# Moving row moments behind the residual sums, and splitting the normalization's apply over two engines, in the first stage of a decoder kernel

## The chip, the cores and the metric

The kernel runs on one core of a Trainium2 chip. The metric is the device time of one execution in microseconds. Each kernel is timed several times; the profile is one further execution, recorded by the hardware profiler.

The engines are named as the profile names them: PE is TensorE (matrix products; PEld its weight loads), DVE is VectorE, ACT is ScalarE, POOL is GpSimd, SP is SyncE, which issues most of the DMAs. Each engine runs its instructions in the order in which they were queued. An instruction that must wait holds up all that is queued behind it on the same engine, and nothing on the others.

## The reference

The program is a decoder of two layers with normalization after each residual sum. Four sequences ("batches") of 512 tokens and width 256 are carried through six blocks, all in float32. Only the first block matters here:

```
K, V, Q = x @ theta_K.T, x @ theta_V.T, x @ theta_Q.T
for each token in order:                      # W, b start at W0, b0
    g = (2/256) * (W @ k + b - v)
    W = W - 0.01 * outer(g, k);  b = b - 0.01 * g
    out = W @ q + b
x = layernorm(x + out)                        # mean and variance over the 256 columns, eps 1e-5
```

The five blocks behind it (attention over a context of 1601 tokens, a routed mixture of eight experts, causal self attention, cross attention with rotary positions, and a dequantized feed-forward block) read that `x`. None of their code is touched.

## The kernel before

A sequence of 512 tokens is held as four tiles of 128 tokens on 128 partitions: `x[b]` is 128 x 4 x 256. `xT[b]` is its transpose, which products need as an operand.

The first stage is the generator `ttt(b)`. The token loop is turned into triangular products over tiles of 128 tokens. One call of the generator runs to its next `yield`, and queues a small piece of work:

- call 1: `to_xT`, eight transposes on PE (L188) and one ACT copy out of PSUM (L196);
- calls 2 and 3: `kT` and `qT`, eight 512-column products each (L202), then an ACT copy (L300);
- calls 4 to 7: for each tile i, the products of kT with kT and qT (fewer columns with each i), a DVE instruction into `gh` (L316), and two POOL instructions (L317, L318);
- call 8: two DVE instructions that start `inv` (L323, L324);
- calls 9 to 20: six levels of inverting the triangular blocks; the first call of a level transposes `inv` (L329), copies it (L331), and masks a product into `mid` (L336), the second adds a product to `inv` (L343);
- calls 21 to 28: for each tile j two calls. The odd one queues a product into `rs` (L367), and, for j > 0, `out_of(j-1)`: a product whose residual sum `r[:, j-1]` is made by DVE (L357). The even one queues the short product of `inv` with `rs`, copied by ACT into `z` (L373);
- call 29: `out_of(3)`, then `normalize`: four `bn_stats` (L107), four `bn_aggr` (L109), a square root on ACT (L98), a reciprocal (L100) and four `tensor_scalar` (L116), all but the root on DVE;
- call 30: `to_xT` of the normalized tiles, for the next stage.

The addition of `b0b` to `x[b]` (L305) is queued on POOL in call 4, but depends only on the transposes of call 1, so POOL may run it early.

The order of the stage is written out by hand: under `manual_schedule` the program order is the queue order. The loop at the end of the stage takes at most two generators forward in turns, one call each per turn, the older first. The second generator starts after the seventh turn, the third after the first has ended, the fourth after the second. In the order so made, the end of the first batch (A) stands with calls 22 and 23 of the second (B), the end of B with calls 6 and 7 of C, the end of C with calls 22 and 23 of D, and D ends alone.

PSUM holds in this stage two double-bank tiles (`wide`, for the transposes and the wide products) and four single banks (`bank`). The tiles of pool `p1` have two buffers, one for each of the two batches under way.

The second stage begins with small products of weights (`w`, `w2T`), then the queries from `xT[0]`. The loads of the next weights are queued on SP behind the end of the first stage, because they reuse its memory. The third to sixth stages follow, PE being the busiest engine in all of them. In a later stage `normalize_apart` normalizes in another way: a DVE instruction makes `nb` = -mean x rstd (L166), and ACT applies scale and shift with Identity (L171).

Of the kernel before, what the change touches and what calls it, by code (L numbers as in the profile page):

```python
# [9 lines left out]
F32 = mybir.dt.float32  # L10
I32 = mybir.dt.int32
BF16 = mybir.dt.bfloat16
AF = mybir.ActivationFunctionType
ALU = mybir.AluOpType
# [3 lines left out]
P = 128  # L18
B, S, D = 4, 512, 256
S2 = 1601  # L20
NT = S // P
# [18 lines left out]
def decoder(ctx: ExitStack, tc: tile.TileContext, a: dict, out: bass.AP):  # L40
    nc = tc.nc

    persist = ctx.enter_context(tc.tile_pool(name="persist", bufs=1))
    small = ctx.enter_context(tc.tile_pool(name="small", bufs=4))
# [10 lines left out]
    def wide():  # L55
        return psum["A"].tile([P, 2, 512], F32, tag="wide", name="wide")

    def bank():
        return psum["B"].tile([P, 512], F32, tag="bank", name="bank")


    x = [persist.tile([P, NT, D], F32, tag=f"x{b}", name=f"x{b}") for b in range(B)]
# [7 lines left out]
    eps5 = persist.tile([P, 1], F32, tag="eps5", name="eps5")  # L70
# [24 lines left out]
    def rstd_of(mv, eps, n=NT):  # L95

        sd = small.tile([P, NT], F32, tag="sd", name="sd")[:, :n]
        nc.scalar.activation(sd, mv[:, :, 1], AF.Sqrt, bias=eps)  # L98
        rs = small.tile([P, NT], F32, tag="rstd", name="rstd")[:, :n]
        nc.vector.reciprocal(rs, sd)  # L100
        return rs

    def moments(r, n=NT):
        st = small.tile([P, NT, 6], F32, tag="st", name="st")
        mv = small.tile([P, NT, 2], F32, tag="mv", name="mv")[:, :n]
        for t in range(n):
            nc.vector.bn_stats(st[:, t, :], r[:, t, :])  # L107
        for t in range(n):
            nc.vector.bn_aggr(mv[:, t, :], st[:, t, :])  # L109
        return mv  # L110

    def normalize(dst, r):
        mv = moments(r)
        rs = rstd_of(mv, eps5)
        for t in range(NT):
            nc.vector.tensor_scalar(  # L116
                dst[:, t, :], r[:, t, :], mv[:, t, 0:1], rs[:, t : t + 1], ALU.subtract, ALU.mult
            )
# [76 lines left out]
    def to_xT(b):  # L195
        nc.scalar.copy(xT[b], transposed(x[b]))  # L196

    def mm(ps, terms):

        n = len(terms)  # L200
        for i, (l, r) in enumerate(terms):
            nc.tensor.matmul(ps, l, r, start=(i == 0), stop=(i == n - 1))  # L202
# [12 lines left out]
    with (  # L215
# [71 lines left out]
        def bc4(t):  # L287
            return t[:, None, :].to_broadcast([P, NT, P])

        def ttt(b):  # L290

            to_xT(b)
            yield
            kq = []
            for n, w in (("kT", thK), ("qT", thQ)):
                ps = wide()
                for o in range(2):
                    mm(ps[:, o, :], [(w[:, c, o * P : (o + 1) * P], xT[b][:, c, :]) for c in range(2)])
                t = p1.tile([P, 2, S], F32, tag=n, name=n)
                nc.scalar.copy(t, ps)  # L300
                kq.append(t)
                yield
            kT, qT = kq

            nc.gpsimd.tensor_tensor(x[b], x[b], b0b[:, None, :].to_broadcast([P, NT, D]), ALU.add)  # L305


            gh = p1.tile([P, NT, 2, S], F32, tag="gh", name="gh")
            dg = p1.tile([P, NT, P], F32, tag="dg", name="dg")
            for i in range(NT):  # L310
                blk = slice(i * P, (i + 1) * P)
                n = slice(i * P, S)
                ps = wide()
                for w, t in enumerate((kT, qT)):
                    mm(ps[:, w, n], [(kT[:, c, blk], t[:, c, n]) for c in range(2)])
                nc.vector.tensor_scalar(gh[:, i, :, n], ps[:, :, n], 1.0, -CSTEP, ALU.add, ALU.mult)  # L316
                nc.gpsimd.tensor_copy(dg[:, i, :], gh[:, i, 0, blk])  # L317
                nc.gpsimd.tensor_tensor(gh[:, i, 1, blk], gh[:, i, 1, blk], lev[:, NLEV, :], ALU.mult)  # L318
                yield


            inv = p1.tile([P, NT, P], F32, tag="inv", name="inv")
            nc.vector.tensor_tensor(inv, dg, bc4(lev[:, 0, :]), ALU.mult)  # L323
            nc.vector.tensor_tensor(inv, inv, bc4(ident), ALU.add)  # L324
            yield
            for l in range(1, NLEV):
                pt = bank()
                for j in range(NT):
                    nc.tensor.transpose(pt[:, j * P : (j + 1) * P], inv[:, j, :], ident)  # L329
                back = p1.tile([P, NT, P], F32, tag="back", name="back")  # L330
                nc.scalar.copy(back, pt.rearrange("p (j q) -> p j q", q=P))  # L331
                pa = bank()
                for j in range(NT):
                    mm(pa[:, j * P : (j + 1) * P], [(dg[:, j, :], inv[:, j, :])])
                mid = p1.tile([P, NT, P], F32, tag="mid", name="mid")
                nc.vector.tensor_tensor(  # L336
                    mid, pa.rearrange("p (j q) -> p j q", q=P), bc4(lev[:, l, :]), ALU.mult
                )
                yield
                pc = bank()  # L340
                for j in range(NT):
                    mm(pc[:, j * P : (j + 1) * P], [(back[:, j, :], mid[:, j, :])])
                nc.vector.tensor_tensor(inv, inv, pc.rearrange("p (j q) -> p j q", q=P), ALU.add)  # L343
                yield

            z = p1.tile([P, NT, D], F32, tag="z", name="z")
            rs = p1.tile([P, NT, D], F32, tag="rs", name="rs")
            r = p1.tile([P, NT, D], F32, tag="r", name="r")

            def out_of(j):  # L350
                ps = bank()
                mm(
                    ps[:, :D],
                    [(qT[:, c, j * P : (j + 1) * P], w0T[:, c, :]) for c in range(2)]
                    + [(gh[:, i, 1, j * P : (j + 1) * P], z[:, i, :]) for i in range(j + 1)],
                )
                nc.vector.tensor_tensor(r[:, j, :], ps[:, :D], x[b][:, j, :], ALU.add)  # L357

            for j in range(NT):
                blk = slice(j * P, (j + 1) * P)  # L360
                ps = bank()
                mm(
                    ps[:, :D],
                    [(xT[b][:, c, blk], merged[:, c, :]) for c in range(2)]
                    + [(gh[:, i, 0, blk], z[:, i, :]) for i in range(j)],
                )
                nc.vector.tensor_tensor(rs[:, j, :], ps[:, :D], b0b, ALU.add)  # L367
                if j > 0:
                    out_of(j - 1)
                yield  # L370
                ps = bank()
                mm(ps[:, :D], [(inv[:, j, :], rs[:, j, :])])
                nc.scalar.copy(z[:, j, :], ps[:, :D])  # L373
                yield
            out_of(NT - 1)
            normalize(x[b], r)
            yield
            to_xT(b)

        ordered.enter_context(tc.manual_schedule())  # L380
        going, waiting, turn = [ttt(0)], [1, 2, 3], 0
        while going:
            for g in list(going):
                if next(g, going) is going:
                    going.remove(g)
            turn += 1
            if waiting and len(going) < 2 and turn >= 7:
                going.append(ttt(waiting.pop(0)))
            if turn == 9:
                clear_rows()  # L390
# [237 lines left out]
    with tc.tile_pool(name="p2", bufs=2) as p2, ExitStack() as ordered:  # L628
# [175 lines left out]
        for i in range(len(steps) + 1):  # L804
            if i + 1 < len(steps):
                b, t = steps[i + 1]
# [11 lines left out]
            if i > 0:  # L818
                b, t = steps[i - 1]
# [1220 lines left out]
```

## Time and profile before

| What | Value |
|---|---|
| Time, three runs | 2365.4, 2371.91, 2372.49 us (median 2371.91) |
| The profiled execution | 2369.97 us, its span 2367.9 us |
| Mean granted PE clock of the span | 0.972 |
| First stage, start to the last transposes | 0 to about 242 us |
| PE busy in 0 to 242 us | 208.41 us |
| DVE, ACT, POOL busy in 0 to 242 us | 81.33, 38.46, 23.22 us |

The span is the time between the first and the last instruction in the profile. "Busy" counts running instructions only. The granted clock is the share of full speed that PE's clock was given: at 0.50 every product takes twice as long. In a timeline line the columns are start (us), duration (us), engine, line, operation, output<-input, shapes, count, and in brackets the engine's idle time before it and what ended that.

### The profile page before, as it was taken

Reading aid. Unit: us, or ns where it says so; the run is one execution under the profiler, and the core shown is the slowest. Engines: PE = TensorE matmul, PEld = TensorE weight load, DVE = VectorE, ACT = ScalarE, POOL = GpSimd, SP = SyncE. Lnnn points to the kernel's source line nnn. Section 1 sums busy time; section 2 is a strip of 40 time slices with the busy share of each in tenths; the row PEclk is TensorE's granted clock in tenths of the full one; section 3 lists DMA queues with packets and bytes.
Section 4 is the critical chain, followed back from the end, with each engine's and each line's share of the span. In section 5 each row is a group of like instructions: output and inputs, shape, how many; then the busy total and the mean of one; then the engine's idle time right before and its main releaser. Section 6 shows DMA issues by size and latency. Waiting matters only on the chain.

```text
span 2367.9 us, 36132 instructions
## 1 busy us (share of the span) xinstructions
PE 2271.9 (96%) x14440; PEld 1287.9 (54%) x14440; DVE 1233.4 (52%) x2918; ACT 1064.2 (45%) x2103; POOL 371.2 (16%) x383
## 2 busy tenths in 40 slices
PE   7899999989999999889999999999999999999998
PEld 4768577768989889633333344333333333333366
DVE  1433334442343443565666676667776776777234
ACT  1111222224555455334555534656656565666730
POOL 1010001121222223426120000211112010000000
PEclk9999999989999999889999988999999999999999
DMA  8400311127877777343131210111110010101000
GB/s 303 181 0 1 134 56 46 46 108 247 348 296 279 282 275 285 112 151 89 60 114 57 84 37 1 42 54 48 69 34 29 25 60 20 60 1 28 23 9 27
DMA packets 77099, 244.13 MB, mean 103 GB/s; under 512 B 11640, under 2 KB 34686, under 8 KB 64638
## 3 DMA queue, kind: packets, MB, share of 16 engines
q1 hardware_dynamic: 59310, 140.39, 17.1%
q0 software_dynamic: 13632, 89.32, 10.0%
q10 hardware_dynamic: 3984, 12.05, 1.5%
q8 instruction: 116, 1.90, 0.3%
q14 instruction: 57, 0.47, 0.1%
HBM read 196.12 MB, written 56.77 MB: 107 GB/s over the span
## 4 chain that ended last, share of the span: by engine, by line
PE 54%; DMA 1%; DVE 1%; ACT 1%; POOL 1%; SPq 0%; issue 0%; DVEq 0%; POOLq 0%; ACTq 0%
PE s L1472 24%; PE one L202 12%; PE po L1499 12%; PE s L202 3%; PE s L1482 1%; PE one L1457 1%; DMA kcd<-in_c_rowkc 1%; PE one L1520 1%; ACT x L171 0%; ACT ex L1486 0%; DMA y<-ys,yrows 0%; DMA cx<-in_ctxT 0%; DVE pm L1429 0%; DVE one L1431 0%; PE one L1541 0%
## 5 line engine op out<-in xcount | busy, mean ns | idle before, releaser
L1486 ACT ACTIVATE ex<-s 128x512 f32<-128x512 f32 (+1 forms) x1062 | 578.2, 594 | 462.4 <-PE s L1472 227.7
L1429 DVE TENSOR_REDUCE pm<-one 128x1 f32<-128x512 f32 x768 | 493.6, 685 | 163.7 <-PE s L1472 107.5
L1472 PE MATMUL s<-q,kc 32*128 32x512 f32 x1612 | 531.2, 641 | 0.8 <-ACT ex L1486 0.8
L202 PE MATMUL one<-kc,qt 32*128 32x512 f32 (+1 forms) x2048 | 485.3, 565 | 0.3 <-DVE pm L1429 0.3
L1472 PEld LDWEIGHTS s<-q,kc 32*128 32x128 f32 x1612 | 166.8, 179 | 204.3 <-issue 172.4
L1499 PE MATMUL po<-ex,v 128*32 128x256 f32 (+3 forms) x2688 | 251.7, 443 | 0.3 <-ACT ot L1512 0.3
L1431 DVE CUSTOM_DVE_ANT_0 one<-one,c_diagq 128x512 f32<-128x512 f32 x256 | 171.9, 716 | 86.1 <-PE one L202 76.6
L1499 PEld LDWEIGHTS po<-ex,v 128*32 128x32 f32 (+1 forms) x2688 | 54.1, 108 | 253.1 <-issue 246.4
L1472 PE MATMUL s<-q,ks 32*128 32x512 f32 x512 | 179.5, 656 | 12.0 <-DVE q L1461 7.2
L202 PEld LDWEIGHTS one<-kc,qt 32*128 32x128 f32 x2048 | 164.9, 189 | 11.7 <-DVE pm L1429 7.9
L202 PE MATMUL one<-ks,qt 32*128 32x512 f32 x512 | 148.2, 656 | 0.0
L202 PE MATMUL bank<-eWo,g 128*128 128x256 f32 x608 | 138.8, 384 | 8.7 <-DVE rb L995 5.4
L202 PE MATMUL wide<-xbT,eWg 128*128 128x128 f32 (+1 forms) x960 | 138.9, 305 | 2.1 <-ACT g L973 2.1
L202 PE MATMUL wide<-xbT,eWi 128*128 128x128 f32 (+1 forms) x960 | 138.7, 305 | 0.9 <-DMA eWi<-in_eWi 0.9
L975 DVE TENSOR_TENSOR g<-g,sg 128x1024 f32<-128x1024 f32 x38 | 46.4, 1223 | 174.5 <-ACT sg L973 165.6
L202 PEld LDWEIGHTS wide<-xbT,eWi 128*128 128x128 f32 x960 | 129.5, 192 | 9.7 <-issue 2.1
L202 PEld LDWEIGHTS wide<-xbT,eWg 128*128 128x128 f32 x960 | 129.8, 194 | 8.9 <-ACT g L973 2.3
L1304 POOL TENSOR_TENSOR raw<-raw,c_cos 128x512 f32<-128x512 f32 (+1 forms) x32 | 35.0, 1095 | 632.5 <-DVE swp L1303 632.5
L202 PEld LDWEIGHTS bank<-eWo,g 128*128 128x128 f32 x608 | 114.4, 192 | 27.8 <-DVE rb L995 9.4
L1472 PEld LDWEIGHTS s<-q,ks 32*128 32x128 f32 x512 | 53.5, 187 | 90.0 <-issue 70.6
L202 PE MATMUL wide<-ctxT,q 128*128 128x512 f32 (+1 forms) x256 | 91.3, 510 | 0.8 <-DVE q L669 0.8
L973 ACT ACTIVATE g<-wide,eWi 128x128 f32<-128x128 f32 (+1 forms) x240 | 72.8, 411 | 38.9 <-PE wide L202 38.1
(346 smaller groups left out, 2955.1 us busy)
## 6 DMA issues: line engine op xcount, KB each, us to landing
xs<-zero SPq DMA_DIRECT2D x32, 512.0 KB
kc<-kcd SPq DMA_DIRECT2D x16, 800.5 KB
eWo<-in_eWo SPq DMA_DIRECT2D x8, 1408.0 KB
eWi<-in_eWi SPq DMA_DIRECT2D x8, 1028.0 KB
eWg<-in_eWg SPq DMA_DIRECT2D x8, 1028.0 KB
qt<-qd SPq DMA_DIRECT2D x32, 256.0 KB
ctxT<-in_ctxT SPq DMA_DIRECT2D x4, 1601.0 KB
kcd<-raw SPq DMA_DIRECT2D x24, 256.0 KB
```

What stands on the lines that cost most here:

```text
L202: nc.tensor.matmul(ps, l, r, start=(i == 0), stop=(i == n - 1))
L973: nc.scalar.activation(dst[:, k, :], pv[:, k, :], func, bias=bias)
L975: nc.vector.tensor_tensor(part, part, dst, ALU.mult)
L1304: eng.tensor_tensor(raw[:, :n], raw[:, :n], cos[:, :n], ALU.mult)
L1429: nc.vector.tensor_reduce(pm[:, t, j, c : c + 1], ps, AX.X, ALU.max)
L1431: nc.vector.tensor_tensor_reduce(out=ps, in0=ps, in1=diagq[:, 384 - t * P : 896 - t * P], scale=1.0, scalar=LOWEST, op0=ALU.add, op1=ALU.m ...
L1457: nc.tensor.transpose(pt[:, t * P : (t + 1) * P], ng.rearrange("p j r -> p (j r)"), ident)
L1472: nc.tensor.matmul(ps[:kn], kt[rows, k * P : k * P + kn], q2[rows, :], start=True, stop=cross)
L1482: nc.tensor.matmul(ps[:, k * P : (k + 1) * P], later_[:, :P], later_[:, P:], start=False, stop=True)
L1486: nc.scalar.activation(ex[:kn, h, :], ps[:kn], AF.Exp)
L1499: nc.tensor.matmul(state["po"][j * 32 : j * 32 + 32, q0:q1], (vals if cross else vself)[b % 2][:kn, k, c0 : c0 + 32], ex[:kn, j % 2, q0:q1 ...
L1520: nc.tensor.transpose(pt[:, t * P : (t + 1) * P], ot[:, t * P : (t + 1) * P], ident)
```

## The change

It touches only `ttt(b)`:

1. The `bn_stats` of a tile stands in `out_of`, right behind the residual sum of that tile. Its tile `st` comes from pool `p1`.
2. A `yield` stands between `out_of(3)` and the rest of the normalization, so that each generator has 31 calls in place of 30: 29 is `out_of(3)`, 30 the rest of the normalization, 31 `to_xT`.
3. The rest of the normalization is written out. The four `bn_aggr`, the square root and the reciprocal stay; DVE adds one small instruction, `nb`. Tiles 0 and 1 are shifted and scaled by ACT with Identity, tiles 2 and 3 by DVE as before.

```
                 nc.vector.tensor_tensor(r[:, j, :], ps[:, :D], x[b][:, j, :], ALU.add)
-
+                nc.vector.bn_stats(st[:, j, :], r[:, j, :])
+
+            st = p1.tile([P, NT, 6], F32, tag="st", name="st")
             for j in range(NT):
...
             out_of(NT - 1)
-            normalize(x[b], r)
+            yield
+
+            mv = small.tile([P, NT, 2], F32, tag="mv", name="mv")
+            for t in range(NT):
+                nc.vector.bn_aggr(mv[:, t, :], st[:, t, :])
+            rstd = rstd_of(mv, eps5)
+            nb = small.tile([P, NT], F32, tag="nb", name="nb")
+            nc.vector.scalar_tensor_tensor(
+                out=nb, in0=mv[:, :, 0], scalar=-1.0, in1=rstd, op0=ALU.mult, op1=ALU.mult
+            )
+            for t in range(2):
+                nc.scalar.activation(
+                    x[b][:, t, :], r[:, t, :], AF.Identity, scale=rstd[:, t : t + 1], bias=nb[:, t : t + 1]
+                )
+            for t in range(2, NT):
+                nc.vector.tensor_scalar(
+                    x[b][:, t, :], r[:, t, :], mv[:, t, 0:1], rstd[:, t : t + 1], ALU.subtract, ALU.mult
+                )
             yield
             to_xT(b)
```

With 31 calls, the end of A stands with calls 22 to 24 of B, C starts beside call 25 of B instead of 24, the end of B stands with calls 5 to 7 of C, the end of C with calls 22 to 24 of D, and D ends alone.

## The prediction

> **What bounds the kernel now.** I read the page first: TensorE is busy for 96% of the span, and the chain that ended last runs mostly over its matmuls. So the change is worth what it takes from TensorE's own lost time in the first stage (0 to 242 us); VectorE and ScalarE time counts only where TensorE waits for it.
>
> ```profile
> span 2367.9 us, 36132 instructions
> ...
> PE 2271.9 (96%) x14440; PEld 1287.9 (54%) x14440; DVE 1233.4 (52%) x2918; ACT 1064.2 (45%) x2103; POOL 371.2 (16%) x383
> ```
>
> Second, TensorE's waits alone between 38 and 250 us (total, times, longest). The first line is what the change is aimed at: the transposes of `to_xT` (L188) wait for the normalized tiles (L116), 9.7 us over four batch ends.
>
> ```profile
> PE wide L188 <- DVE x L116: 9.7, 4, 4.0
> PE bank L329 <- DVE inv L324: 5.3, 4, 3.3
> ```
>
> Third, the timeline of the first batch's end. I call the batches A to D, and A29 the 29th call of A's generator.
>
> ```profile
> 104.28 0.59 PE L202 MATMUL bank<-rs,inv 128*128 128x256 f32 x2
> 104.49 0.42 DVE L357 TENSOR_TENSOR r<-bank,x 128x256 f32<-128x256 f32 x1 [2.17 <-PE bank L202]
> 104.83 1.40 DVE L107 BATCH_NORM_STATS2 st<-r 128x6 f32<-128x256 f32 x4
> 106.14 0.36 DVE L109 BATCH_NORM_AGGREGATE mv<-st 128x2 f32<-128x6 f32 x4
> 106.58 1.28 ACT L98 ACT_TABLE_LOAD   x1 [5.17 <-DVE mv L109]
> 107.87 0.30 ACT L98 ACTIVATE sd<-mv,eps 128x4 f32<-128x4 f32 x1
> 108.08 0.35 ACT L373 COPY z<-bank 128x256 f32<-128x256 f32 x1
> 108.20 0.18 DVE L100 RECIPROCAL rstd<-sd 128x4 f32<-128x4 f32 x1 [1.70 <-ACT sd L98]
> 108.42 1.38 DVE L116 TENSOR_SCALAR x<-r,mv,rstd 128x256 f32<-128x256 f32 x4
> ...
> 108.88 2.30 PE L188 MATMUL wide<-ident,x 128*128 128x128 f32 x8 [4.00 <-DVE x L116]
> ```
>
> Only B22's product (104.28) covers a serial chain over two engines. After it the eight transposes take 2.30 us; undisturbed ones elsewhere take about 1.04. The reason is in the table by stretches (duration; busy us; then granted clock before the last two columns):
>
> ```profile
> 104.00:115.00 11.00, 7.00 (x24) 5.36 (x23) 4.00 (x15) 2.85 (x4) 0.00 (x0) 0.69 0.00 0
> ...
> 141.00:149.00 8.00, 6.53 (x32) 5.35 (x30) 4.80 (x17) 1.31 (x2) 1.40 (x4) 0.79 0.00 0
> ...
> 200.00:215.00 15.00, 14.65 (x85) 13.04 (x85) 4.88 (x9) 1.89 (x4) 0.00 (x0) 1.00 0.00 0
> 216.00:224.00 8.00, 5.33 (x20) 3.96 (x19) 3.58 (x14) 1.57 (x3) 0.00 (x0) 0.79 0.01 2
> ...
> 237.00:248.00 11.00, 7.18 (x25) 4.86 (x24) 4.31 (x16) 2.59 (x3) 0.25 (x2) 0.69 0.40 140
> ```
>
> A quiet stretch is granted 1.00. Around the ends of A, B, C and D the clock is at 0.50 for (1 - 0.69) x 2 x 11 = 6.8 us, 3.4, 3.4 and 6.8 us. An end thus costs its wait and, for the work inside, half the time at half clock.
>
> **The change, part by part.** *Moments early.* Three of four `bn_stats` (0.35 us apart, from 1.40 for four) leave each end, 1.05 us less. They go behind the sums of tiles 0 to 2, just ahead of the partner's `inv` update (L343). That one waits 0.47 us for TensorE there (r at 99.71, L343 at 100.60), so 0.35 fits: cost 0, and 0.35 each if that wait were gone. *Half the apply on ScalarE.* Two `tensor_scalar` become two Identity activations. The form exists in a later stage: L171, 591 ns, four in 2.07 us, so two end 1.08 us after they start, beside two VectorE tiles in 0.70. A new `nb` costs 0.16 (L166 when POOL is quiet). From the end of the reciprocal to the last tile: 0.16 + about 0.08 of hand-over + 1.08 = 1.3 us, against 1.4 now. No gain there; the gain is in what is taken off before it. *One turn later.* Each generator has 31 calls instead of 30. No DMA is added or moved in a queue. POOL work stays in order. The SP loads behind the stage (from 241.13 us, after the last tile) just move with its end.
>
> *A's end.* The order on TensorE becomes A29, B22, B23, A31, B24. B22 ends at 104.71. B23 is 12 matmuls of 0.215 us, 2.58 us, to 107.29; its first part needs z(0), whose copy now precedes the square root in ScalarE's queue and ends at 105.3. VectorE: sum to 104.91, moments to 105.2, aggregates to 105.54; ScalarE's table load and root to 107.16; reciprocal 107.38, nb 107.54. ScalarE tiles at 108.19 and 108.68, VectorE tiles by 108.2. Transposes wait 0.95 us at 107.29 and 0.4 between tiles, and end at 109.5. B23's sums are queued on VectorE behind the apply, and B24 waits for rs(1): ready at 108.6, in time. B24 started at 115.22 and now at 109.5: **5.7 us**.
>
> Here a rule is weighed. The Trainium skill, "TensorE: Matmul & The Clock Gate", Part 1, has the clock halved after an idle free-running window of 3.4 us and restored by a busy one. By it the 1.35 us left at A would cost nothing, and of the four ends only A's 4.0 us wait could have halved it. The rows differ: waits of 2.67 (C), 1.53 (D) and 1.47 us (B) were followed by 3.4 or 6.8 us at half. One of 1.59 us, at 41.6, was not. The measurement decides: I charge A half a window's loss, 0.5 x 1.7 = **-0.85** (ends 0 and -1.7).
>
> *Junction of B and C.* C starts one B call later, so C's transposes are followed by B26's short product (0.43 us) where B25 (3.45 us) stood. C2 needs xT(C): 0.2 to ScalarE, 1.01 copy, 0.05 back, less 0.43: **-0.83** of new wait.
>
> *B's end.* Cover is now C5 (2.58) and C6 (1.72), but B30's aggregates stand on VectorE behind C5's `gh` (0.96), which waits for C5's matmuls. Counted from C6's last matmul at 0: C5 ends -1.72, gh -0.56, aggregates -0.20, root 0.14, reciprocal 0.36, nb 0.5; tiles complete at 1.63, transposes run from 1.18 to 2.45. Now they end at 3.52 (142.35 to 145.87). Gain 1.07; C6's `gh` behind the apply delays nothing (C7's buffer is free at 2.0). With full clock C7 and D1 gain about 0.9 more; with half clock the transposes lose about 0.4. Ends 0.7 and 2.0, I take the middle: **1.35**. The next wait, for L324 (2.71 us there, beside POOL's L305 of 2.63), stays.
>
> *C's end.* As A's, with no table load. D23 ends at 219.4, tiles at 218.2 to 219.55, transposes end 220.35 at full clock. D24 moves from 225.23 to 220.35: **4.9 us**. All 2.67 us of wait and the 1.7 us of half clock go.
>
> *D's end.* No partner, so nothing covers. 1.05 us less moments plus 0.1 less apply; but the later second tile (0.5 after the first) leaves seven transposes behind it: at half clock they end at 241.5, against 242.27: **0.75** (1.5 if the clock holds).
>
> Sum: 5.7 - 0.85 - 0.83 + 1.35 + 4.9 + 0.75 = **11.0 us**. The profiled execution took 2369.97 us (span 2367.9 and 2.07 around it): 2359.0. The median of the runs shown is 1.94 higher, so I predict **2361**. With all unknown terms at their ends the gain is 9.5 to 13.3. By the page's rule (no half clock left anywhere) it would be 13.3, or 2358.6. The three runs lie 7.1 us apart; with half of that the likeliest case's own range is 2355 to 2366. 0.3% is 7.1 us, about what a measurement can tell here: 2364.8 is the border.
>
> **The rivals.** *The stalls stay in the clock* (0.12). The remaining waits are short, but the rows show 1.5 us to be enough. If A, the junction and C each still lose a window (1.7 each) and B and D give their low ends: 5.7 - 1.7 - 0.83 - 1.7 + 4.9 - 1.7 + 0.7 + 0.75 = 6.1, or 2366. For: the 1.47 us case. Against: C keeps no wait, the junction 0.83, and gaps of 0.88 us (66.35) left the clock alone.
>
> *Gained here, lost later* (0.11). Over the span (1 - 0.972) x 2 x 2367.9 = 133 us are at half clock; the first 242 us, at 0.96, hold 19, so 113 us or some 33 windows lie behind. If four more fall, 4 x 1.7 = 6.8 us are eaten: 2367.7. Against: these stretches shift as a whole, since nothing after 242 us is tied to the launch, and the clear of `xs` is over by 84 us.
>
> *Slower: the table of ScalarE* (0.07). The trace shows a copy right behind a square root with no load (108.08), but never Identity there. Were it missing from the set with Sqrt, every end would load twice: seven loads more than now. At the row's 1.283 us that is 9.0, with a window more at A, B and C 14.1: 3.1 slower. "ScalarE: Activation LUTs" ("What ACT_TABLE_LOAD costs") prices a switch at 2.66 us with a drain: 18.6 + 5.1, which is 12.7 slower, 2385. It becomes slower by over 0.3% from 1.85 us a switch. The row, with the root running 0.01 us after the load, shows no drain behind it; and the same page ("Table sets") counts identity with copy among the functions in every set. So I hold it unlikely.
>
> **How the numbers follow.** The likeliest case has 0.70. Faster: that less 0.03 for its weak end, plus 0.05 of the clock case, 0.72. Same: 0.03 + 0.07 + 0.09 = 0.19. Slower: 0.07 and 0.02 of the later loss, 0.09. The range runs from the low end, 2355, to 2372, which takes in both rivals on the near side and leaves out the table case.
>
> **What would show it.** Right: waits of L188 for x fall from 9.7 us to about 4 (A 1.3, B 1.6, C none, D 1.5), C's stretch is at clock 1.00, C2's matmuls wait 0.8 us for xT, the stage's last transposes start about 11 us earlier. Wrong: table loads ahead of Identity, half clock at C's end, or a stage that ends 11 us earlier and a span that doesn't.

## The result, and the profile after

The changed kernel takes 2358.51 us (median of 17 runs, 2350.81 to 2364.43) against 2365.4 us for the kernel before (17 runs, 2360.69 to 2372.49). The ratio is 0.9966 with a 95% interval of 0.9956 to 0.9977: faster by about 8.0 us (0.0034 x 2365.4), between 5.4 and 10.4. The two medians alone differ by 6.9 us, which lies within that interval. The prediction was 11.0 us and 2361. The median of before had been 2371.91 over the first three runs; over 17 it is 6.5 lower. That and a gain 3 too large nearly cancel, so the predicted time fits better than the predicted gain.

The head of the page after:

```profile
span 2360.1 us, 36135 instructions
...
PE 2265.0 (96%) x14440; PEld 1281.5 (54%) x14440; DVE 1232.9 (52%) x2914; ACT 1068.4 (45%) x2111; POOL 371.0 (16%) x383
```

The span is 7.8 us shorter. ScalarE ran eight instructions more (2111 against 2103), the eight Identity, and VectorE four fewer (2914 against 2918): eight `tensor_scalar` less, four `nb` more. No table load was added. TensorE's waits from 38 to 240 us (total, times, longest):

```profile
PE bank L329 <- DVE inv L324: 5.3, 4, 3.3
PE wide L188 <- ACT x L389: 3.6, 6, 1.1
...
PE wide L202 <- ACT xT L196: 1.8, 2, 1.1
```

The wait for the normalized tiles fell from 9.7 to 3.6 us (about 4 was forecast). It is now put down to ScalarE's tiles. The junction's new wait for `xT` is in the third line: 1.1 us of it is at the stage's end, as before, and 0.67 is new. The wait for L324 is what it was.

The end of A in the timeline after:

```profile
104.81 0.37 ACT L375 COPY z<-bank 128x256 f32<-128x256 f32 x1 [3.51 <-PE bank L202]
...
105.18 0.36 DVE L382 BATCH_NORM_AGGREGATE mv<-st 128x2 f32<-128x6 f32 x4
...
105.62 1.28 ACT L98 ACT_TABLE_LOAD   x1 [0.44 <-DVE mv L382]
...
106.91 0.30 ACT L98 ACTIVATE sd<-mv,eps 128x4 f32<-128x4 f32 x1
...
107.53 0.73 DVE L393 TENSOR_SCALAR x<-r,mv,rstd 128x256 f32<-128x256 f32 x2
107.71 1.09 ACT L389 ACTIVATE x<-r,nb,rstd 128x256 f32<-128x256 f32 x2 [0.50 <-DVE nb L385]
...
108.36 0.33 PE L188 MATMUL wide<-ident,x 128*128 128x128 f32 x1 [1.01 <-ACT x L389]
...
108.86 0.98 PE L188 MATMUL wide<-ident,x 128*128 128x128 f32 x7 [0.16 <-ACT x L389]
```

The copy of z(0) now runs ahead of the root, and no load stands between the root and Identity. TensorE waits 1.01 us and loses a little more between the first two tiles; the seven other transposes run at full speed. Two of the stretches that were shown of before (the granted clock is the third column from the end):

```profile
104.00:115.00 11.00, 9.83 (x52) 8.02 (x50) 4.49 (x16) 4.69 (x8) 0.32 (x1) 1.00 0.01 1
...
200.00:215.00 15.00, 14.60 (x79) 12.54 (x79) 6.76 (x20) 3.10 (x7) 0.00 (x0) 1.00 0.00 0
```

The ends of B, C and D, with B's and D's cut to where they stand now:

```profile
141.00:152.00 11.00, 7.51 (x28) 5.11 (x28) 4.76 (x4) 2.08 (x3) 3.30 (x3) 0.69 0.01 1
216.00:224.00 8.00, 8.00 (x39) 7.04 (x38) 1.70 (x4) 1.40 (x3) 0.00 (x0) 1.00 0.01 2
228.00:238.00 10.00, 6.80 (x24) 4.86 (x24) 2.41 (x11) 3.69 (x5) 0.25 (x2) 0.66 0.51 178
```

The ends of A and C are at full clock. Behind B there are still (1 - 0.69) x 2 x 11 = 6.8 us at half clock, as much as B's end and the wait behind it had together before, and D's end keeps its 6.8. In the first stage of every profile here the half clock lasts 3.41 us or a whole multiple of it; one such piece is called a window below. As work at half clock takes twice as long, a full window costs up to 1.7 us.

To compare stages I took five points at which the same work lies behind TensorE in both orders: the start of B1's transposes, of B24's product, of C's first transposes of `inv`, of D24's product, and of the first product with `gram`. The stretch between the first and the last is called "the stretch" below. Launch-time differences ahead of it (up to 3.6 us between profiles) are so left out.

| Part of the stretch (us) | before | after | gain | forecast |
|---|---|---|---|---|
| B1 to B24 (end of A) | 76.27 | 70.83 | 5.44 | 5.7 - 0.85 |
| B24 to C's `inv` (junction, end of B) | 37.15 | 36.23 | 0.92 | -0.83 + 1.35 |
| C's `inv` to D24 (end of C) | 72.86 | 69.64 | 3.22 | 4.9 |
| D24 to `gram` (end of D) | 25.73 | 25.27 | 0.46 | 0.75 |
| the stretch | 212.01 | 201.97 | 10.0 | 11.0 |

Behind the stretch nothing was changed, yet the lead of 10.2 us at `gram` is not kept evenly. Matched product by product it is 9.9 at 925 us of the trace after, 7.5 at 1052, 9.3 at 1303, 7.7 at 1377, 9.6 at 1676, 8.0 at 2161 and 7.8 at the end. It moves in steps of 0.3 to 2 us both ways.

### The profile page after: what moved, and what is told of

The parts are those of the page before. It is cut to its first block, busy times and chain, and to the rows that moved or that the text cites. A ratio compares the mean times of both kernels' runs of the same rounds, so it can differ in the third digit from the quotient of the medians.

```text
span 2360.1 us, 36135 instructions
## 1 busy us (share of the span) xinstructions
PE 2265.0 (96%) x14440; PEld 1281.5 (54%) x14440; DVE 1232.9 (52%) x2914; ACT 1068.4 (45%) x2111; POOL 371.0 (16%) x383
## 4 chain that ended last, share of the span: by engine, by line
PE 54%; DMA 2%; ACT 1%; DVE 1%; POOL 1%; issue 0%; SPq 0%; DVEq 0%; ACTq 0%; POOLq 0%
PE s L1491 24%; PE po L1518 12%; PE one L202 12%; PE s L202 3%; PE s L1501 1%; PE one L1476 1%; PE one L1539 1%; DMA kcd<-in_c_rowkc 1%; DMA kcd<-raw 1%; ACT x L171 0%; ACT ex L1505 0%; DMA y<-ys,yrows 0%; DMA cx<-in_ctxT 0%; DVE pm L1448 0%; DVE one L1450 0%
```

## The experiments

All stretches below are measured as above, each from one profile, so a difference of a window or two between single profiles can be chance. The times are medians, and each ratio is to the kernel before on the same chip.

| Run | Stretch, us | TensorE's wait for x, us | Ratio, 95% interval |
|---|---|---|---|
| before | 212.0 | 9.7 | 1 |
| the change | 202.0 | 3.6 | 0.9966 (0.9956 to 0.9977) |
| e1 turn only | 207.3 | 4.9 | 0.9988 (0.9974 to 1.0003) |
| e2 moments only | 209.3 | 6.3 | 0.9985 (0.9972 to 0.9999) |
| e3 split only | 211.1 | 11.7 | 1.0017 (1.0002 to 1.0032) |
| e4 change without split | 201.6 | 1.9 | 0.9966 (0.9951 to 0.9980) |
| e5 the change again | 201.8 | 3.5 | 0.9962 (0.9949 to 0.9975) |
| e6 addition in call 9 | 209.1 | 3.7 | 0.9999 (0.9984 to 1.0013) |
| e7 aggregates first | 199.1 | 3.0 | 0.9963 (0.9947 to 0.9979) |
| e8 no split, e6 and e7 | 212.0 | 1.3 | 0.9982 (0.9968 to 0.9996) |
| e9 addition behind tile 0 | 198.7 | 3.7 | 0.9951 (0.9936 to 0.9966) |
| e10 no split, e7 and e9 | 195.4 | 1.2 | 0.9957 (0.9941 to 0.9973) |
| e11 e10 with the early product | 192.2 | 0.6 | 0.9921 (0.9902 to 0.9940) |
| e12 change with the early product | 196.6 | 2.7 | 0.9944 (0.9925 to 0.9963) |

**The parts alone.** My theory was that the added turn pays, since it puts the partner's work over the normalization. The rivals were the early moments and the split. The expectations of e1 to e4 name the start of the product with `gram` as their marker; it stood at 242.8, 246.3, 246.7 and 238.5 us. But B1 had started 1.9 to 3.5 us earlier in these four profiles than in that of before, ahead of anything that was edited, so I read the stretch instead. By the marker as written, e3 would have met its rival (248 or earlier); by the stretch it gains 0.9 us.

e1, the turn alone:

```
             out_of(NT - 1)
+            yield
             normalize(x[b], r)
             yield
```

> The kernel before with one more yield ahead of the whole normalization, and nothing else. Marker: the start of the first product with gram (251.0 us before, 240.8 us with the change). Theory (the turn gives cover): A gains 4.6 us, the junction of B and C costs 0.9, B's end loses 0.9 (moments too now stand behind C5's gh), C gains 3.8, D nothing: 6.6, marker at 244.4. Rival (the early moments carry it): the chain is as long as before, the marker gains under 3 us, 248 or later.

e2, the moments alone:

```
                 nc.vector.tensor_tensor(r[:, j, :], ps[:, :D], x[b][:, j, :], ALU.add)
+                nc.vector.bn_stats(st[:, j, :], r[:, j, :])
...
-            normalize(x[b], r)
+            mv = small.tile([P, NT, 2], F32, tag="mv", name="mv")
+            for t in range(NT):
+                nc.vector.bn_aggr(mv[:, t, :], st[:, t, :])
+            rstd = rstd_of(mv, eps5)
+            for t in range(NT):
+                nc.vector.tensor_scalar(
+                    x[b][:, t, :], r[:, t, :], mv[:, t, 0:1], rstd[:, t : t + 1], ALU.subtract, ALU.mult
+                )
             yield
```

> The kernel before with the moments of each tile behind its residual sum; no added turn, all four tiles on VectorE. Theory (the turn gives cover): each end is 1.05 us shorter, 4.2 in all, and most of the half clock stays: marker at 246.8, and at 245 if B's end keeps its clock. Rival (the early moments carry it): marker gains 7 us or more, 244 or earlier.

e3, the split alone:

```
-            normalize(x[b], r)
+            mv = moments(r)
+            rstd = rstd_of(mv, eps5)
...
+            for t in range(2):
+                nc.scalar.activation(
+                    x[b][:, t, :], r[:, t, :], AF.Identity, scale=rstd[:, t : t + 1], bias=nb[:, t : t + 1]
+                )
+            for t in range(2, NT):
+                nc.vector.tensor_scalar(
+                    x[b][:, t, :], r[:, t, :], mv[:, t, 0:1], rstd[:, t : t + 1], ALU.subtract, ALU.mult
+                )
```

> The kernel before with tiles 0 and 1 applied on ScalarE with Identity, 2 and 3 on VectorE; moments and turn as before. Theory: no gain, since nb and two Identity (1.3 us) take what four VectorE tiles take (1.4), and the second tile comes late: marker at 251 to 252. Rival (the split carries it): marker gains 3 us or more, 248 or earlier.

e4, the change without its split:

```
-            nb = small.tile([P, NT], F32, tag="nb", name="nb")
...
-            for t in range(2, NT):
+            for t in range(NT):
                 nc.vector.tensor_scalar(
```

> The changed kernel with all four tiles applied on VectorE again, and no nb. Theory: the split is no part of the gain; the tiles come in the order in which the transposes take them, so 0.2 us earlier at A, B and C and 0.5 at D: marker at 239.9. Rival (the split carries it): marker 3 us or more later than 240.8.

TensorE's wait for the tiles in the four (the first line of e1, then e2, e3 and e4):

```profile
PE wide L188 <- DVE x L116: 4.9, 3, 2.0
```

```profile
PE wide L188 <- DVE x L383: 6.3, 4, 3.2
```

```profile
PE wide L188 <- ACT x L383: 11.7, 6, 4.4
```

```profile
PE wide L188 <- DVE x L385: 1.9, 3, 0.7
```

By waits, the turn takes 4.8 us off, the moments 3.4, and the split adds 2.0 alone and 1.7 (3.6 against 1.9) inside the change. So neither the split nor the moments carry the gain alone. That the turn gives more than the moments rests on these waits and on one profile each: in time, the turn alone is at 0.9988 (0.9974 to 1.0003) and the moments alone at 0.9985 (0.9972 to 0.9999), which doesn't tell them apart.

By the stretch, the turn gains 4.7 (6.6 was expected): 4.76 at A (4.6), -0.30 at junction and B (-1.8), 2.59 at C (3.8), and -2.37 at D, where the added turn has no partner to change places with, but where this profile has 17 us at half clock, from 228.7 to 245.7, in place of 6.8. The moments gain 2.7 (4.2); A's end stayed at half clock for 6.8 us there, behind its 3.2 us wait.

Together the two alone make 7.4, the change 10.0. The difference lies at D, and it goes with the clock: e1 lost 2.37 there and e2 0.90, with 17 and 10.2 us at half clock, where the change gained 0.46 with 6.8. Over the three parts ahead of D the two alone make 10.7 and the change 9.6, so together they give no more than the sum of the two.

In times the split alone is slower by 0.17% (0.02 to 0.32). In e4 the stretch is 0.4 us shorter than with the split (0.9 was expected), and the times of the two can't be told apart. That e3's stretch is 0.9 shorter than before's while its waits are 2.0 longer shows the same thing from the other side: in that profile A's end had one window (106.3 to 109.7) where before's had two, and B's end and the wait behind it had one together (147.2 to 150.6) where before's had two.

**The change again, and the steps of B's end.** e5 is the changed kernel, unedited.

> The changed kernel itself, once more, beside the three that follow. From the second batch's first transposes to the first product with gram it took 201.96 us (before 212.0). Theory (the half clock comes in whole windows of a free grid, so one profile's stretch moves by steps of about 1.7 us while the waits stay): waits for x of 3.6 us again, the stretch 202 plus or minus 3.4. Rival (the clock follows the waits alone): the stretch within 0.5 us of 201.96.

The stretch was 201.84, within 0.13 of the first. The half-clock stretches fell in the same places, from 144.8 instead of 144.9. By its number the stated rival fits. But this run could not decide: B1 also started at the same time, 38.87 and 38.84, so the place of the work against the windows, which my theory needs to vary, happened to be nearly the same. The profiles of e1 to e4 started there at 35.5 to 37.0, with windows at other places. Within each profile the starts of its half-clock stretches in this stage lie whole multiples of 3.41 us apart; what is left over on dividing them by 3.41 us differs between profiles (0.5 us in e3, 1.6 in the change, 3.4 in e1). What that place does to one and the same wait is read from all profiles in the next section.

e6 moves POOL's addition, which runs beside L324 of C, to call 9:

```
-            nc.gpsimd.tensor_tensor(x[b], x[b], b0b[:, None, :].to_broadcast([P, NT, D]), ALU.add)
...
             nc.vector.tensor_tensor(inv, inv, bc4(ident), ALU.add)
             yield
+            nc.gpsimd.tensor_tensor(x[b], x[b], b0b[:, None, :].to_broadcast([P, NT, D]), ALU.add)
```

> The changed kernel with POOL's addition of b0b to x queued in call 9 instead of call 4. Theory (B's end gained only 0.9 us because the wait for L324, 2.71 us beside that addition, keeps the clock down right behind it): L324 takes 0.7 us there, TensorE's wait falls from 3.3 to 1.3 us, the stretch from the second batch's first transposes to gram falls from 202.0 by 2.0, and by up to 3.4 more where the half clock goes too: 196.6 to 200. Rival (L324 is slow for another reason, or the addition only slows other VectorE work): 202 within 1.

It lost nearly the whole gain, which neither the theory nor the rival had said. The instructions on `inv` in the change (minimum, median, maximum ns), then in e6:

```profile
L323 DVE TENSOR_TENSOR inv<-dg,lev x4: 681/804/930, 39.8 to 173.2; 128x512 f32<-128x512 f32 x4
L324 DVE TENSOR_TENSOR inv<-inv,ident x4: 692/693/2709, 40.8 to 173.9; 128x512 f32<-128x512 f32 x4
```

```profile
L320 DVE TENSOR_TENSOR inv<-dg,lev x4: 929/1468/2005, 39.4 to 177.3; 128x512 f32<-128x512 f32 x4
L321 DVE TENSOR_TENSOR inv<-inv,ident x4: 691/1701/2714, 40.4 to 179.3; 128x512 f32<-128x512 f32 x4
```

My placing was wrong: in call 9 the addition waits for nothing but its turn on POOL, so it started right behind the last `gh` work of its own batch, which is just when VectorE starts that batch's `inv`. One collision became one in each batch, and TensorE's wait for `inv` went from 5.3 to 9.9 us. It says nothing against the collision; it multiplies it.

e7 puts the aggregates ahead of the yield:

```
             out_of(NT - 1)
-            yield
-
             mv = small.tile([P, NT, 2], F32, tag="mv", name="mv")
             for t in range(NT):
                 nc.vector.bn_aggr(mv[:, t, :], st[:, t, :])
+            yield
+
             rstd = rstd_of(mv, eps5)
```

> The changed kernel with the four aggregates ahead of the added yield. Theory (at B's end they stand behind C5's gh on VectorE): the root runs before gh ends, reciprocal 0.6 us sooner, TensorE's wait for x at B's end 1.04 to 0.4 us; ends of A, C and D unchanged. Rival (the queue place costs nothing): the wait at B's end stays 1.0.

The end of B in the timeline of e7:

```profile
134.72 0.36 DVE L380 BATCH_NORM_AGGREGATE mv<-st 128x2 f32<-128x6 f32 x4
...
136.50 0.96 DVE L316 TENSOR_SCALAR gh<-wide 128x768 f32<-128x768 f32 x1 [1.42 <-PE wide L202]
...
137.37 0.17 DVE L100 RECIPROCAL rstd<-sd 128x4 f32<-128x4 f32 x1
...
138.57 0.33 PE L188 MATMUL wide<-ident,x 128*128 128x128 f32 x1 [0.39 <-ACT x L389]
```

The aggregates no longer wait for C5's `gh`, and B's wait is 0.39 us in place of 1.04, as expected; all of it in the sum, 3.6 to 3.0. The stretch is 2.7 shorter than in e5, with 3.4 us of half clock less behind B and 3.4 less at D, so most of it is clock. The times show no difference to the change that could be told (0.9963 and 0.9962).

e8 joins e4, e6 and e7:

> The change with all four tiles on VectorE, the aggregates ahead of the yield, and POOL's addition in call 9. Theory: the sum of the parts, 0.4 + 0.6 + 2.0 to 5.4 = 3 to 6.4 us below the change. Rival (the waits only move): the time of the change within 1.5 us.

Its stretch is as long as before's, 212.0, with e6's wait: TensorE waits 10.0 us for `inv`. Its time (0.9982) is nearer to the kernel before than the change's (0.9962 beside it), though the intervals just overlap.

e9 gives the addition a place that it must wait for:

```
-            nc.gpsimd.tensor_tensor(x[b], x[b], b0b[:, None, :].to_broadcast([P, NT, D]), ALU.add)
...
                 nc.gpsimd.tensor_tensor(gh[:, i, 1, blk], gh[:, i, 1, blk], lev[:, NLEV, :], ALU.mult)
+                if i == 0:
+                    nc.gpsimd.tensor_tensor(x[b], x[b], b0b[:, None, :].to_broadcast([P, NT, D]), ALU.add)
```

> The changed kernel with POOL's addition of b0b to x queued behind the first tile's gh work of the same batch (call 4, after L317 and L318 for i = 0), so that it waits for that gh and can't run beside the partner's start of inv. Theory (L324 is slow only beside that addition): all four L324 take 0.69 us, TensorE's wait for them 5.3 to about 3.3 us, the stretch from the second batch's first transposes to gram 201.9 to 196.5-199.9, the time 2 to 5 us below the change. Rival (the addition slows whatever VectorE does beside it): gh, mid or inv updates grow in its place and the time is that of the change within 1.5 us.

TensorE's waits in e9, and its second instruction on `inv` (the lines are one lower than in the change):

```profile
PE wide L188 <- ACT x L388: 3.7, 6, 1.1
PE bank L328 <- DVE inv L323: 3.2, 4, 1.6
```

```profile
L323 DVE TENSOR_TENSOR inv<-inv,ident x4: 691/692/692, 39.0 to 167.3; 128x512 f32<-128x512 f32 x4
```

All four now take 0.69 us, and the wait falls by 2.1. Beside the moved addition run `gh`, one residual sum and its moments, none of them longer than elsewhere (0.96, 0.42 and 0.43 us); the means of `gh`, `mid` and the `inv` updates are those of the change (824, 692 and 687 ns). The half clock behind B is gone, too. Part by part the stretch is 2.0 us shorter from B24 to C's `inv` and 2.8 from there to D24, against the change: 4.9 in all, and then 1.6 longer at D, whose half clock in this profile lasted 13.7 us. In time, over five runs, e9 can't be told from the change (0.9951, up to 0.9966).

**D's end, and a faster version.** e10 joins e4, e7 and e9. e11 and e12 add the early product, which gives TensorE work while D is normalized:

```
+        wT = p2in.tile([P, 2, D], F32, tag="wT", name="wT")
...
             out_of(NT - 1)
+            if b == B - 1:
+                pw = wide()
+                for o in range(2):
+                    mm(pw[:, o, :D], [(w2T[:, h, o * P : (o + 1) * P], w1[:, h, :]) for h in range(2)])
...
+            if b == B - 1:
+                nc.vector.tensor_copy(wT, pw[:, :, :D])
             yield
             to_xT(b)
...
-        wT = p2.tile([P, 2, D], F32, tag="wT", name="wT", bufs=1)
...
-        ps = wide()
-        for o in range(2):
-            mm(ps[:, o, :D], [(w2T[:, h, o * P : (o + 1) * P], w1[:, h, :]) for h in range(2)])
-        nc.vector.tensor_copy(wT, ps[:, :, :D])
```

> The change with four tiles on VectorE, the aggregates ahead of the yield, and the addition behind the first tile. Theory: 0.4 + 0.6 + 2.0 to 5.4 us below the change, ratio to the kernel before 0.994 to 0.9955. Rival (the waits only move): 0.996 to 0.997 as the change.

> The run before with the product of w and w2T, which opens the second stage, queued behind the last batch's out_of(3), so that TensorE has work while the last tiles are normalized. Theory (D's end and its half clock lie on the path): 4 to 6 us below the run before it, ratio 0.9915 to 0.9935. Rival (D's end is hidden by what follows): ratio as the run before it.

> The changed kernel with that product early, and nothing else. Theory: D's end keeps no 7 us of half clock, the stretch to gram is 4 to 6 us shorter than 201.9. Rival: within 1 us of it.

In e12 the stretch is 196.6, 5.4 less than the change's 202.0, all of it in the last part (19.92 instead of 25.27), and no half clock is left at D. So D's end was on the path. By the trace, TensorE's waits in this part fell from 3.75 to 1.5 us, and the half clock had held 5.6 us of work, so it cost about 2.8 (an estimate: half of that), more than the 1.3 us wait for the tiles. e10's stretch, 195.4, is 6.6 below the change (3 to 6.4 was expected), but in time it can't be told from e9 or from the change. e11, with the product early on top of e10, has the lowest ratio, 0.9921, or 18.6 us below before (0.0079 x 2356.98, the median of before beside it). By the medians it is 15.1: one of its six runs, at 2330.3, lies 11 us below the others. From e12, 0.7 us away by the medians, it can't be told. TensorE's largest waits left in it:

```profile
PE bank L329 <- DVE inv L324: 3.3, 4, 1.6
PE bank L329 <- DVE inv L343: 2.1, 6, 0.3
```

Its stretch is 3.2 us shorter than e10's, where 4 to 6 was expected; the gain in time over e10 (0.0036, or 8.5 us; 5.7 by the medians) is larger. The intervals are each about 4 us wide to either side, so that difference isn't settled.

## Why the prediction was right or wrong

*The mechanism was right.* The partner's work now lies over the normalization at A and C. The times in the timeline at A are within 0.2 us of those worked out: transposes from 108.36 (108.24) and B24 at 109.68 (109.5). C's end keeps no wait and no half clock. The split gives nothing, as the 1.3 against 1.4 us said; with the order of the tiles it costs 0.4 (e4, one profile). The 0.35 us of early moments hid in the 0.47 us wait of L343: from the start of `r` to L343 it is 0.89 us at A, before and after.

*The end of A* was charged 0.85 for a half window, taken between 0 and 1.7. It cost nothing: the clock stayed at 1.00. Here the rule of the Trainium skill that the prediction weighed ("TensorE: Matmul & The Clock Gate", Part 1), by which only an idle window brings the clock down, was nearer than the row I followed. At D of the same profile it was not: waits of 0.5 and 1.1 us were followed by 6.8 us at half.

*What fell short lies behind B's end.* I gave B 1.35 and C 4.9 as if they were separate, and wrote that the wait for L324 "stays". It stayed, at 3.3 us, but more half clock stood behind it. Before, the clock fell twice in this place, once behind B's wait (145.0 to 148.5) and once behind L324's (151.9 to 155.3), 3.4 us each:

```profile
149.00:156.00 7.00, 3.68 (x16) 3.15 (x16) 3.97 (x3) 1.60 (x2) 2.66 (x2) 0.76 0.00 0
```

```profile
152.37 1.12 PE L329 MATMUL bank<-ident,inv 128*128 128x128 f32 x4 [3.32 <-DVE inv L324]
```

After, the clock was 1.00 until 144.9, and at half from there to 151.7, behind L324's wait:

```profile
142.71 2.59 POOL L305 TENSOR_TENSOR x<-x,b0b 128x1024 f32<-128x1024 f32 x1
143.14 2.71 DVE L324 TENSOR_TENSOR inv<-inv,ident 128x512 f32<-128x512 f32 x1
145.90 1.12 PE L329 MATMUL bank<-ident,inv 128*128 128x128 f32 x4 [3.28 <-DVE inv L324]
```

Most of this lies behind the point that ends B's part, so it is booked to C: 3.22 instead of 4.9. C's end itself came out nearly as forecast: from D22 to D24 TensorE took 8.84 us before and 4.17 after, 4.67 less. The other 1.45 is the longer half clock, which held 5.84 us of work in C's part where it had held 2.91. B's and C's parts together gained 4.14, where 5.42 was forecast.

That B's shorter wait made L324's dearer is not shown. In e7 B's wait is shorter still (0.39), L324's the same (3.28), and behind it stands one window. What goes with the length, over the eleven profiles in which TensorE waits 3.3 to 3.4 us for C's `inv`, is where that wait lies against the windows. In before, e3, e6 and e7 its last 0.1 to 0.5 us lay behind the fall of the clock, and the half clock lasted 3.4 us; in the other seven, the change among them, 0.8 to 1.5 us did, and it lasted 6.8. So one and the same wait cost one window or two, and which of the two the profiled pair got looks like chance: the launch shifts that place, and so does every edit ahead of it, and no run moved the windows alone. The wait itself is what the fall needs: in e9, e10 and e11, with L324 at 0.69 us and a wait of 1.3 to 1.4 left, there is no half clock here, and C's part gains 6.06 in e9.

*D's end* was right in kind and 0.3 too high.

*The whole time* gained 8.0 (5.4 to 10.4), the stretch 10.0 in one profile and 10.2 in the other. The second rival, gained here and lost later, describes the profiled pair, in which 2.4 us were lost behind the stage. But all kernels here share the work behind that product, and over their profiles the time from it to the end is between 2105 and 2121 us, without an order by edit: 2116.9 before, 2119.3 and 2120.7 with the change, 2106.0 in e1, 2116.7 in e4. It goes with the clock back there: from 2105.5 us with 86.7 at half clock (e12) to 2120.7 with 110.6 (e5), with a correlation of 0.95 over the 14 profiles. A loss of 2 us that belongs to the change is not shown, and the interval of the times holds 10.0 as well. What remains open is how much of the 2 us is real.

*The table rival* fell: one load at L98 in the stage as before, and Identity right behind `nb` with none.

## What to carry to other kernels

Cover a serial normalization by giving it a turn of its own beside another batch's work, and look at what is queued on its engines in that turn; splitting its last step over two engines helps little when the consumer needs the tiles in order. Price a wait on TensorE together with the clock behind it, and when a wait shrinks, look at the next one on the line: here the half clock behind B went only when L324's wait was shortened as well (e9). Don't read a gain of a window or so from one profile. An instruction queued later doesn't run later unless it waits for something: to move it in time, put it behind a dependence.

## What the runs showed of the hardware

VectorE's sum of two tiles in SBUF took 0.69 us alone and 2.71 beside POOL's addition of 2.6 us (e5, e9), while `gh` and a residual sum (e9) and `mid` (e6), which take an input from PSUM, kept their times beside the same addition. The Trainium skill ("SBUF — State Buffer", "SBUF: two separate sides") describes such a pair as sharing a port under an exclusive lock, the later one waiting out the earlier. The numbers agree: 2.71 is POOL's remaining 2.16 us (142.71 + 2.59 less 143.14) and 0.55 to run.

In the profile after, the clock went to half behind a TensorE wait of 1.1 us at D, which eight products of one column and a wait of 0.5 stand just ahead of, and before behind waits of 1.5 us at B and D; not, after, behind the 1.01 us at A, the 1.04 at B or 1.6 us at 41.5. No length of a single wait divides these cases. Once down it stayed for one window of 3.41 us or for two, three (e2 at D), four (e9 at D) or five (e1 at D). With D's wait filled by one product (e12), it didn't fall there at all.
